# Graph attention on one Trainium2 core: score tiles of 256 nodes and eight heads in place of 128 nodes and sixteen, and an output of 64 matmuls of one form

## The chip, the cores and the metric

The kernel runs on one core of one Trainium2 chip. The core has five engines that run side by side: TensorE (matmuls; in profiles PE, and PEld for its loads of weights), VectorE (DVE), ScalarE (ACT), GpSimd (POOL) and SyncE (SP), which here only issues DMA transfers. SBUF is the on-chip memory, PSUM the banks that matmuls add into. The metric is the device time of one launch in microseconds, as a median of several runs. For a matmul the profile writes the form of the array that it uses, rows by weights: 128\*32 is a tile of all 128 rows and 32 weights, and four such tiles fill the array; 32\*64 and 32\*32 are smaller tiles, of which eight and sixteen fill it.

## The reference

Sixteen graphs (B) of 512 nodes (N) with 512 features. Every node attends to the first 20 nodes of its graph (ng), in two directions d, with 16 heads of 32 features; masks and biases come from 11 edge labels. Cut to what matters:

```python
def _gat_attention(self_feat, cond_adj, label_bias, Wq, bq, Wk, bk, Wout, bout):
    kv = self_feat[:, :ng]
    qh = (self_feat @ Wq.T + bq).reshape(B, N, H, dh)
    kh = (kv @ Wk.T + bk).reshape(B, ng, H, dh)
    aff = jnp.einsum('bnhd,bmhd->bnhm', qh, kh) * (1.0 / np.sqrt(dh))
    mask = cond_adj[:, :, None, :] > 0
    aff = jnp.where(mask, aff, NEG) + label_bias[:, :, None, :]
    w = jax.nn.softmax(aff, axis=-1)
    out_t = jnp.einsum('bnhm,bmf->bnhf', w, kv)
    out = jnp.einsum('bnhf,hgf->bnhg', out_t, Wout) + bout.reshape(H, F // H)
    return out.reshape(B, N, F)
...
self_feat = vcq @ W_self.T + b_self
output = self_feat
for d in range(2):
    A = adj_f if d == 0 else jnp.swapaxes(adj_f, 1, 2)
    A = A[:, :, :NONGT, :]
    cond = A.sum(-1)
    vb = A @ w_bias + b_bias
    output = output + _gat_attention(self_feat, cond, vb, Wq[d], bq[d], Wk[d], bk[d], Wout[d], bout[d])
rel = jax.nn.relu(output)
return exp_v + rel
```

All of it is in float32.

## The kernel before

A setup phase of roughly the first 90 us folds the weights. The keys of all graphs are multiplied with the query weights beforehand (`g`: for each graph and head, 19 vectors, the difference of each key to the first), the values with the output weights (`bd_d` in DRAM), the query bias gives one term for each head and key (`cq_d`). After that a loop runs over the graphs, `b`, and in each over four tiles of nodes, `nt`. Everything stands in an order written out by hand (`manual_schedule`), engine by engine; transfers that must not start too early are held `behind` an instruction.

For one graph the loop does this.

The self features `sf` (512 features by 512 nodes) come from seven block products (`product`, into the banks `ps_a`, `ps_c`, `ps_d`), which VectorE joins (`partial`, `joined`). They are made one graph ahead.

`scores(b, nt, g, bank)` multiplies self features by keys. A score tile has 128 partitions in four quarters of 32, and each quarter is a column tile of TensorE: in a matmul the weights are 32 nodes of `sf`, and 152 columns (4 heads, 2 directions, 19 keys) move past them. Before the change quarter `a` holds the heads 4a to 4a+3, and all four quarters hold the same 32 nodes; a tile thus holds 128 nodes and all sixteen heads, in two banks of two halves each.

`mask_mul`, `mask_count` and `mask_sum` make the additive mask `add` of 256 nodes, 128 nodes on the partitions and two such blocks side by side. A score tile needs the mask of each node in the partition and column where that node stands, so `mask_spread` copies it there on ScalarE into `both`: for each of the four quarters and each of four blocks of 32 nodes one copy of 32 partitions by 80, sixteen copies for 256 nodes. `full_add` (GpSimd) adds the mask and the bias term `cq` to a tile of 640 columns. `weigh` (VectorE) adds the scores from PSUM, takes the maximum and subtracts it; `expo` is ScalarE's exponential; `normal` sums (VectorE) and divides (GpSimd); `turn` is VectorE's transpose of 32 by 32 blocks into `wt`, after which the partitions hold keys.

`attend(b, banks)` is the output: `vd` holds the values as weights, `wt` moves past them, and the result lands in four banks `ps_o`. Of a row quarter (32 of the 128 partitions) come 4 heads. Each head has 40 keys in `wt`, so that heads lie across the blocks of 32: the blocks 1 and 3 belong to two heads each and are taken by matmuls of 64 weights, the others by matmuls of 32 weights. `finish` adds `sf` (VectorE, four additions), applies bias and relu (ScalarE); `residual` adds x (GpSimd) and `store` sends the result. The output of graph b-1 is made in graph b, in tile 2.

The last graph is handled apart: the self features plus bias plus x (`biased`) are put into the banks by an identity matmul (`put_self`), the output follows in two parts (384 nodes, then 128), and VectorE takes it out with a maximum against x (`end`), after which `send` stores it.

```python
for first, runs in ((True, ((1, 2, 1), (5, 2, 3))), (False, ((0, 1, 0), (3, 1, 2), (4, 1, 2), (7, 1, 4)))):
    for at, n, j in runs:
        for a in range(HL):
```

These three lines are the order of the output's matmuls: block of 32 values `at`, `n` such blocks (32 or 64 weights), column block `j` of `wt`, and innermost the row quarter `a`.

## Time and profile before

| what | value |
|---|---|
| runs shown | 580.59, 581.49, 582.52 us; median 581.49 |
| span of the profiled execution | 578.9 us (core 0, mean granted TensorE clock 0.998) |
| one graph in the middle of the loop | 30.5 us |
| transfers | 123.26 MB, mean 213 GB/s |

The page has one time for the profiled execution, its span, from the first to the last instruction; the runs' times are measured around the whole launch and are longer. In the profile's rows a group is written as line, engine, operation, output <- input, shapes and count. A row of the timeline gives start, duration, engine, line, operation and count, and in brackets how long the engine was idle before it and what ended that. PEld rows are the loads of weights, which run beside the matmuls. The duration of a matmul is modelled, the start is recorded, so that the distance from start to start is the safer reading.

```profile
PEclk9999999999999999999999999999999999999999
DMA  8998997867777767777676777566666766674404
```

The page's slices show that the clock was at full speed in all forty of them, and the DMA engines busy some 70% of the time.

### The profile page before, as it was taken

To read this page: it belongs to the slowest core of one execution; us is meant where nothing else is said; L and a number is where in the kernel's file an instruction comes from. 1 tells how busy PE (TensorE), PEld (TensorE's weight loads), DVE (VectorE), ACT (ScalarE), POOL (GpSimd) and SP (SyncE) were. 2 spreads that over 40 slices of the span, in tenths; PEclk is the share of its full clock that TensorE was granted. 3 is DMA by queue.
4 is the path that set the end of the run, shared out by engine and by line. 5 is a ranking of instruction groups with operands and counts; after the bars stand their busy time and mean duration, and the time that the engine had idled before them with its cause. 6 is when DMAs were issued, how large, how long until landed. Compare 5 with 4: busy or idle time off the path is not lost.

```text
span 578.9 us, 31006 instructions
## 1 busy us (share of the span) xinstructions
PE 572.2 (99%) x13508; PEld 434.1 (75%) x13508; DVE 492.9 (85%) x790; ACT 393.6 (68%) x1162; POOL 404.6 (70%) x383
## 2 busy tenths in 40 slices
PE   9999999999999999999999999999999999999996
PEld 6544458888878787878778787877887878787873
DVE  0675776979898989898999999898989898989896
ACT  1234554687878777778786868687887877777571
POOL 2726986658586776858585867776858677785874
PEclk9999999999999999999999999999999999999999
DMA  8998997867777767777676777566666766674404
GB/s 315 382 396 283 333 361 233 237 195 219 209 233 185 220 187 204 213 185 228 167 220 166 222 166 220 164 206 180 204 193 192 195 192 189 192 208 111 147 19 147
DMA packets 98788, 123.26 MB, mean 213 GB/s; under 512 B 18877, under 2 KB 66969, under 8 KB 96605
## 3 DMA queue, kind: packets, MB, share of 16 engines
q1 hardware_dynamic: 96268, 117.54, 67.8%
q0 software_dynamic: 1392, 2.43, 1.8%
q8 instruction: 106, 1.74, 1.3%
q10 hardware_dynamic: 992, 1.31, 0.6%
q14 instruction: 30, 0.24, 0.1%
HBM read 82.30 MB, written 40.24 MB: 212 GB/s over the span
## 4 chain that ended last, share of the span: by engine, by line
PE 98%; DVE 1%; issue 0%; DVEq 0%
PE ps_s L366 46%; PE ps_a L284 19%; PE ps_c L284 9%; PE ps_o L436 6%; PE ps_d L284 5%; PE ps_v L658 3%; PE ps_k L598 3%; PE ps_kv L541 1%; PE ps_o L813 1%; PE ps_warm L500 1%; PE ps_nz L214 0%; PE ps_s L355 0%; PE _g(2, 2, 0, 14, 16)0_845 L692 0%; PE _g(0, 2, 0, 14, 16)0_448 L692 0%; PE g(3, 2, 0, 14, 16)0_1055 L692 0%
## 5 line engine op out<-in xcount | busy, mean ns | idle before, releaser
L366 PEld LDWEIGHTS ps_s<-g,sf 128*32 128x32 f32 x8192 | 263.6, 110 | 21.9 <-issue 14.8
L366 PE MATMUL ps_s<-g,sf 128*32 128x152 f32 x8192 | 278.1, 293 | 0.7 <-issue 0.7
L338 ACT COPY both<-add 32x80 f32<-32x80 f32 x512 | 130.9, 256 | 60.9 <-DVE add L329 55.1
L418 POOL TENSOR_TENSOR s<-s,sm 128x640 f32<-128x640 f32 x63 | 80.4, 1275 | 96.8 <-DVE sm L417 52.5
L345 POOL TENSOR_TENSOR full<-cq,both 128x640 f32<-128x640 f32 x64 | 100.3, 1568 | 26.9 <-issue 20.9
L318 ACT ACTIVATE prod<-adj,wb_sb 128x80 f32<-128x80 int32 x330 | 112.4, 432 | 0.0
L393 ACT ACTIVATE s<-s 128x640 f32<-128x640 f32 x63 | 46.5, 738 | 56.0 <-DVE s L388 55.6
L450 POOL TENSOR_TENSOR o<-o,x 128x512 f32<-128x512 f32 x60 | 76.3, 1293 | 0.0
L380 DVE TENSOR_TENSOR full<-ps_s,full 128x608 f32<-128x608 f32 x63 | 48.6, 772 | 22.5 <-PE ps_s L366 19.4
L284 PE MATMUL ps_a<-t,ws_s 128*32 128x246 f32 x1024 | 59.8, 371 | 0.0
L416 DVE TENSOR_REDUCE sm<-s 128x32 f32<-128x640 f32 x63 | 50.8, 807 | 10.5 <-ACT s L393 10.3
L384 DVE TENSOR_REDUCE ps_s<-full 128x32 f32<-128x640 f32 x63 | 52.2, 828 | 2.2
L425 DVE STREAM_TRANSPOSE wt<-s 128x640 f32<-128x640 f32 x63 | 52.8, 838 | 0.6 <-POOL s L418 0.6
L388 DVE TENSOR_TENSOR s<-full,ps_s 128x640 f32<-128x640 f32 x63 | 51.5, 818 | 1.1
L290 DVE SCALAR_TENSOR_TENSOR sf<-nz,qw,ps_a 128x246 f32<-128x246 f32 x128 | 51.5, 443 | 0.1
L284 PEld LDWEIGHTS ps_a<-t,ws_s 128*32 128x32 f32 x1024 | 34.4, 110 | 16.8 <-issue 0.8
L329 DVE TENSOR_REDUCE add<-prod 128x80 f32<-128x960 f32 x32 | 36.8, 1150 | 7.4 <-ACT prod L318 4.0
L447 ACT ACTIVATE o<-o,bo 128x512 f32<-128x512 f32 x60 | 38.3, 713 | 0.6 <-DVE o L445 0.6
L249 POOL TENSOR_TENSOR t<-x,t 128x492 f32<-128x492 f32 x32 | 36.8, 1151 | 1.3
L436 PE MATMUL ps_o<-wt,vd 32*32 32x512 f32 (+5 forms) x816 | 36.9, 578 | 0.0
L249 POOL TENSOR_TENSOR t<-x 128x492 f32<-128x492 f32 x32 | 36.8, 1151 | 0.0
L445 DVE TENSOR_TENSOR o<-ps_o,sf 128x512 f32<-128x512 f32 x60 | 36.7, 668 | 0.0
(225 smaller groups left out, 715.8 us busy)
## 6 DMA issues: line engine op xcount, KB each, us to landing
g<-g_d SPq DMA_DIRECT2D x60, 304.0 KB
g_d<-st SPq DMA_DIRECT2D x16, 1064.0 KB
out_T<-o SPq DMA_DIRECT2D x60, 256.0 KB
xn<-in_xn SPq DMA_DIRECT2D x56, 256.0 KB
x<-in_xT SPq DMA_DIRECT2D x56, 256.0 KB
adj<-in_adj SPq DMA_DIRECT2D x60, 220.0 KB
nz<-nz_d SPq DMA_DIRECT2D x14, 256.0 KB
wk<-in_wkT SPq DMA_DIRECT2D x2, 1024.0 KB
```

What stands on the lines that cost most here:

```text
L249: done["xsum"] = nc.gpsimd.tensor_sub(t, one, two)
L284: nc.tensor.matmul(to, lhs, x[:, k], start=start, stop=stop, skip_group_check=n != 2)
L290: done["partial"] = nc.vector.scalar_tensor_tensor(to[:, i], nzs[b][:, half(l)], qw[:, 2 * f + i, b : b + 1], parts[b, "a"][i][:, :HN], AL ...
L318: nc.scalar.activation(p[:, :, l], a[:, :, l], AF.Identity, scale=wb_sb[:, l : l + 1])
L338: done["spread"] = nc.scalar.copy(adds[b, h][bass.ts(a, R), :, g], add[r].rearrange("p (t m) -> p t m", t=2))
L345: done["full"] = nc.gpsimd.tensor_add(f, cqs[b].unsqueeze(1).to_broadcast(shape), adds[b, nt // 2][:, nt % 2].unsqueeze(2).to_broadcast(sh ...
L366: nc.tensor.matmul(to, sfs[b][:, k, bass.ds(nt * P + (2 * g + j) * R, R)], of, start=(onto is None and k == 0 and (whole or j == 0)), stop ...
L384: nc.vector.tensor_reduce(mx, f, AX.X, ALU.max)
L418: done["normal"] = nc.gpsimd.tensor_mul(s, s, sm.unsqueeze(3).to_broadcast(full))
L425: nc.vector.transpose(wts[b][:, nt], s.rearrange("p a h m -> p (a h m)"))
L436: nc.tensor.matmul(banks[a][bass.ds(at // 2 * DH, n * DH)].rearrange("p (t n) -> p t n", n=32), vd[r, bass.ds(at * DH, n * DH)], wt[r, :, ...
L450: nc.gpsimd.tensor_add(o[:, c], o[:, c], xs[b][:, c])
```

## The change

A score tile now holds 256 nodes and eight heads. Quarter `a` takes the head group `a // 2 * 2 + nt % 2` and, of every block of 64 nodes, the half `a % 2`; the tiles 0 and 1 share the first 256 nodes, the tiles 2 and 3 the others. The count and size of the score matmuls stay. Since a half of the partitions now has one set of heads, with 64 consecutive nodes, the mask is copied in four pieces of 64 partitions by 80 for 256 nodes. `load_cq` brings the bias terms of eight heads to each half, in two transfers of 64 partitions in place of four of 32, and `load_values` the values of two head groups to each row quarter, four transfers as before, of twice the size.

The output has one form of matmul: 32 rows, 32 weights, 256 columns, for each of two blocks of a head (`i`), two head groups (`c`), four heads (`e`) and four row quarters (`a`). Bank `a` now holds what row quarter `a` gives: two head groups for every second block of 32 nodes. `finish` and the last graph's `end` therefore read and write runs of 32 elements (`spread_out`), and the last graph's steps are split where a bank changes from one head group to the other.

On TensorE, this is the middle of the output of one graph before the change (names: line, operation, output <- input, weights by columns):

```order
L436 MATMUL ps_o_0_3137<-wt_2508,vd_2989 64x512
L436 MATMUL ps_o_1_3138<-wt_2508,vd_2989 64x512
L436 MATMUL ps_o_2_3139<-wt_2508,vd_2989 64x512
L436 MATMUL ps_o_3_3140<-wt_2508,vd_2989 64x512
L436 MATMUL ps_o_0_3137<-wt_2508,vd_2989 32x512
L436 MATMUL ps_o_1_3138<-wt_2508,vd_2989 32x512
L436 MATMUL ps_o_2_3139<-wt_2508,vd_2989 32x512
L436 MATMUL ps_o_3_3140<-wt_2508,vd_2989 32x512
```

and this is where the output of one graph begins after it, with the product and the score tile ahead:

```order
L285 MATMUL ps_c_2201<-x_1608,ws_s 32x246 x16
L369 MATMUL ps_s_1_2385<-g_1960,sf_2061 32x152 x64
L443 MATMUL ps_o_0_2493<-wt_1850,vd_2359 32x256
L443 MATMUL ps_o_1_2494<-wt_1850,vd_2359 32x256
L443 MATMUL ps_o_2_2495<-wt_1850,vd_2359 32x256
L443 MATMUL ps_o_3_2496<-wt_1850,vd_2359 32x256
```

The 24 matmuls of two widths have become 64 of one width, half as many columns each, with the four banks still in turn; the stages around them stand where they stood.

On ScalarE, a stretch of the loop before:

```order
L193 ACTIVATE xn_1_2571,rs_2720<-xn_1_2571 128x512 x2
L338 COPY both_0_2733<-add_0_2731 32x2x40 x16
L393 ACTIVATE s_3_2852<-s_3_2852 128x640
L318 ACTIVATE prod_1_2866<-adj_1_2437,wb_sb 128x80 x11
L338 COPY both_1_2996<-add_1_2994 32x2x40 x8
L393 ACTIVATE s_0_3010<-s_0_3010 128x640
```

and the same stretch after:

```order
L194 ACTIVATE xn_1_2571,rs_2720<-xn_1_2571 128x512 x2
L338 COPY both_0_2733<-add_0_2731 64x2x40 x4
L396 ACTIVATE s_3_2840<-s_3_2840 128x640
L319 ACTIVATE prod_1_2854<-adj_1_2397,wb_sb 128x80 x11
L338 COPY both_1_2984<-add_1_2982 64x2x40 x2
L396 ACTIVATE s_0_2992<-s_0_2992 128x640
```

The copies of the mask stand at the same places, a quarter as many, each on 64 partitions.

The diff, cut to its core:

```diff
     def load_cq(b, ins=None):
-        cqs[b] = load.tile([P, HL, S], F32, tag="cq", name=f"cq{b}")
-        for a in range(HL):
+        cqs[b] = load.tile([P, 2, HL, S], F32, tag="cq", name=f"cq{b}")
+        for p in range(2):
             behind(nc.sync.dma_start(
-                cqs[b][bass.ts(a, R)].rearrange("p h m -> p (h m)"),
-                cq_d[b : b + 1, bass.ts(a, HL)].rearrange("b h d m -> b (h d m)").partition_broadcast(R),
-            ), ins if a == 0 else None)
+                cqs[b][bass.ts(p, P // 2)].rearrange("p c h m -> p (c h m)"),
+                cq_d[b : b + 1, bass.ts(p, H // 2)].rearrange("b h d m -> b (h d m)").partition_broadcast(P // 2),
+            ), ins if p == 0 else None)
...
-        vds[b] = gp.tile([P, HL, 2, DH], F32, tag="vd", name=f"vd{b}", bufs=1)
-        for c in range(C):
+        vds[b] = gp.tile([P, 2, HL, 2, DH], F32, tag="vd", name=f"vd{b}", bufs=1)
+        for a in range(HL):
+            of = bd_d[b >= EARLY][a // 2 * 2 : a // 2 * 2 + 2, b if b < EARLY else b - EARLY]
             behind(nc.sync.dma_start(
-                vds[b][bass.ts(c, 32)].rearrange("p e i g -> p (e i g)"), bd_d[b >= EARLY][c, b if b < EARLY else b - EARLY].rearrange("r e i g -> r (e i g)")
-            ), ins if c == 0 else None)
+                vds[b][bass.ts(a, R)].rearrange("p c e i g -> p c (e i g)"), of.rearrange("c r e i g -> r c (e i g)")
+            ), ins if a == 0 else None)
...
         done["masks"] = nc.vector.tensor_reduce(add, prods.pop((b, h)), AX.X, ALU.add)
-        adds[b, h] = msk.tile([P, 2, HL, S], F32, tag="both", name=f"both{b}_{h}")
+        adds[b, h] = msk.tile([P, 2, 2, S], F32, tag="both", name=f"both{b}_{h}")
...
         for a in quarters:
-            for g in range(HL):
-                r = bass.ts(g, R)
-                done["spread"] = nc.scalar.copy(adds[b, h][bass.ts(a, R), :, g], add[r].rearrange("p (t m) -> p t m", t=2))
+            p, u = bass.ts(a // 2, P // 2), a % 2
+            done["spread"] = nc.scalar.copy(
+                adds[b, h][p, :, u], add[bass.ts(u, P // 2)].rearrange("p (t m) -> p t m", t=2)
+            )
...
         done["full"] = nc.gpsimd.tensor_add(
-            f, cqs[b].unsqueeze(1).to_broadcast(shape),
-            adds[b, nt // 2][:, nt % 2].unsqueeze(2).to_broadcast(shape),
+            f, cqs[b][:, nt % 2].unsqueeze(1).to_broadcast(shape),
+            adds[b, nt // 2].rearrange("p t u m -> p (t u) m").unsqueeze(2).to_broadcast(shape),
         )
...
                 for a in range(HL):
-                    to, of = bank[bass.ts(a, R), bass.ts(j, WD // HL)], keys[:, k, a]
+                    at = nt // 2 * 2 * P + (2 * g + j) * 2 * R + a % 2 * R
+                    to, of = bank[bass.ts(a, R), bass.ts(j, WD // HL)], keys[:, k, a // 2 * 2 + nt % 2]
                     if onto is not None:
...
                     nc.tensor.matmul(
-                        to, sfs[b][:, k, bass.ds(nt * P + (2 * g + j) * R, R)], of,
+                        to, sfs[b][:, k, bass.ds(at, R)], of,
                         start=(onto is None and k == 0 and (whole or j == 0)), stop=(k == C - 1 and (whole or j == 1)),
...
         if nt == 0:
-            wts[b] = work.tile([P, NT, W], F32, tag="wt", name=f"wt{b}")
-        nc.vector.transpose(wts[b][:, nt], s.rearrange("p a h m -> p (a h m)"))
-
-    def attend(b, banks, tiles=slice(0, NT), start=True, stop=True):
-
-
-        wt = wts[b][:, tiles].rearrange("p t (g w) -> p (t g) w", g=HL)
-        vd = vds[b].rearrange("p e i g -> p (e i g)")
-        for first, runs in ((True, ((1, 2, 1), (5, 2, 3))), (False, ((0, 1, 0), (3, 1, 2), (4, 1, 2), (7, 1, 4)))):
-            for at, n, j in runs:
-                for a in range(HL):
-                    r = bass.ts(a, R)
-                    nc.tensor.matmul(
-                        banks[a][bass.ds(at // 2 * DH, n * DH)].rearrange("p (t n) -> p t n", n=32),
-                        vd[r, bass.ds(at * DH, n * DH)], wt[r, :, bass.ts(j, 32)],
-                        start=start and first, stop=stop and not first,
-                    )
+            wts[b] = work.tile([P, 2, 2, W], F32, tag="wt", name=f"wt{b}")
+        nc.vector.transpose(wts[b][:, nt % 2, nt // 2], s.rearrange("p a h m -> p (a h m)"))
+
+    def spread_out(t, a):
+
+        return t[:, a // 2 * 2 : a // 2 * 2 + 2].rearrange("p c (n u r) -> p c u n r", u=2, r=R)[:, :, a % 2]
+
+    def attend(b, banks, spans, start=True, stop=True):
+
+
+        for i in range(2):
+            for c, at, lo, hi in spans:
+                for e in range(HL):
+                    for a in range(HL):
+                        r = bass.ts(a, R)
+                        wt = wts[b][:, c, lo:hi].rearrange("p l (g w) -> p (l g) w", g=HL)
+                        nc.tensor.matmul(
+                            banks[a][bass.ts(e, DH), bass.ds(at, (hi - lo) * P)].rearrange("p (n r) -> p n r", r=R),
+                            vds[b][r, c, e, i], wt[r, :, bass.ts(e * S // 32 + i, 32)],
+                            start=start and i == 0 and at == 0, stop=stop and i == 1, skip_group_check=True,
+                        )
...
-        for c in range(C):
-            done["add", c] = nc.vector.tensor_add(o[:, c], banks[c], sfs[b][:, c])
+        for a in range(HL):
+            done["add", a] = nc.vector.tensor_add(
+                spread_out(o, a), banks[a].rearrange("p (c n r) -> p c n r", c=2, r=R), spread_out(sfs[b], a)
+            )
         for c in range(C):
...
     with tc.manual_schedule():
-        def put_self(banks, lo, hi, q):
-
-            nc.tensor.matmul(
-                banks[q][:, : (hi - lo) * P], ident, biased[:, q, lo * P : hi * P], start=True, stop=False
+        def put_self(bank, a, ns):
+
+            for lo in range(ns.start, ns.stop, N // 2):
+                n = min(N // 2, ns.stop - lo)
+                nc.tensor.matmul(
+                    bank[:, bass.ds(lo - ns.start, n)], ident, biased[:, a, bass.ds(lo, n)],
+                    start=lo == ns.start, stop=False, skip_group_check=True,
+                )
+
+        def put_bias(c):
+            nc.scalar.activation(
+                biased[:, c // 2 * 2 : c // 2 * 2 + 2].rearrange("p u (c n r) -> p n c u r", c=2, r=R)[:, :, c % 2],
+                sfs[b][:, c].rearrange("p (n u r) -> p n u r", u=2, r=R), AF.Identity, bias=bo[:, c : c + 1],
             )
+
+        def add_x(a, lo):
+            for c in range(2):
+                at = slice(max(lo, c * N // 2), (c + 1) * N // 2)
+                if at.start < at.stop:
+                    nc.gpsimd.tensor_add(
+                        biased[:, a, at].rearrange("p (n r) -> p n r", r=R),
+                        biased[:, a, at].rearrange("p (n r) -> p n r", r=R),
+                        spread_out(xs[b], a)[:, c, at.start // R - c * 8 :],
+                    )
...
                         for c in (0, 1):
-                            nc.gpsimd.tensor_add(biased[:, c], biased[:, c], xs[b][:, c])
+                            add_x(c, 0)
                     if b > 0:
                         banks = [bank(f"ps_o{b - 1}_{q}", q) for q in range(4)]
-                        attend(b - 1, banks)
+                        attend(b - 1, banks, ((0, 0, 0, 2), (1, N // 2, 0, 2)))
                         o = work.tile([P, C, N], F32, tag="o", name=f"o{b - 1}")
...
                     for q in range(4):
-                        put_self(most, 0, NT - 1, q)
+                        put_self(most[q], q, slice(0, N - P))
                     s = soft.tile(full, F32, tag="s", name=f"s{b}_{nt}", bufs=3)
...
         rest += [bank(f"ps_o{b}_{q}_2", q - 2) for q in (2, 3)]
-        for lo, hi, banks in ((0, NT - 1, most), (NT - 1, NT, rest)):
-            if banks is rest:
-                for q in range(4):
-                    put_self(rest, lo, hi, q)
-            attend(b, [t[:, : (hi - lo) * P] for t in banks], slice(lo, hi), False)
-
-        def end(lo, hi, banks, q):
-
-            ns = slice(lo * P, hi * P)
-            nc.vector.tensor_max(o_last[:, q, ns], banks[q][:, : (hi - lo) * P], xs[b][:, q, ns])
-
-        def send(queue, c, lo, hi, n=2):
-            queue.dma_start(out_b[:, c : c + n, lo * P : hi * P], o_last[:, c : c + n, lo * P : hi * P])
-
-        w = (NT - 1) * P
-        nc.scalar.activation(o_last[:, 3, :w], most[3][:, :w], AF.Relu)
-        behind(nc.gpsimd.tensor_add(o_last[:, 3, :w], o_last[:, 3, :w], xs[b][:, 3, :w]), done["half"])
-        for q in range(3):
-            end(0, NT - 1, most, q)
-            send(nc.scalar if q == 1 else nc.sync, q, 0, NT - 1, 1)
-        send(nc.scalar, 3, 0, NT - 1, 1)
-        for q in range(4):
-            end(NT - 1, NT, rest, q)
-            if q % 2:
-                send(nc.scalar if q == 1 else nc.sync, q - 1, NT - 1, NT)
+        attend(b, most, ((0, 0, 0, 2), (1, N // 2, 0, 1)), False)
+        for a in range(HL):
+            put_self(rest[a], a, slice(N - P, N))
+        attend(b, rest, ((1, 0, 1, 2),), False)
+
+        pieces = ((0, 0, 8, 0), (1, 0, 4, N // 2))
+        last = (1, 4, 8, 0)
+
+        def end(bank, a, piece):
+
+            c, lo, hi, at = piece
+            nc.vector.tensor_max(
+                spread_out(o_last, a)[:, c, lo:hi],
+                bank[:, bass.ds(at, (hi - lo) * R)].rearrange("p (n r) -> p n r", r=R),
+                spread_out(xs[b], a)[:, c, lo:hi],
+            )
+
+        def send(queue, q, lo=0, hi=N):
+            queue.dma_start(out_b[:, q, lo:hi], o_last[:, q, lo:hi])
+
+        for c, lo, hi, at in pieces:
+            to = spread_out(o_last, 3)[:, c, lo:hi]
+            nc.scalar.activation(to, most[3][:, bass.ds(at, (hi - lo) * R)].rearrange("p (n r) -> p n r", r=R), AF.Relu)
+            behind(nc.gpsimd.tensor_add(to, to, spread_out(xs[b], 3)[:, c, lo:hi]), done["half"])
+        for a in range(2):
+            for piece in pieces:
+                end(most[a], a, piece)
+        send(nc.sync, 0)
+        send(nc.scalar, 1, 0, N // 2)
+        for piece in pieces:
+            end(most[2], 2, piece)
+        send(nc.sync, 2)
+        send(nc.scalar, 3, 0, N // 2)
+        for a in range(HL):
+            end(rest[a], a, last)
+            if a % 2:
+                send(nc.scalar if a == 1 else nc.sync, a, N // 2, N)
```

10 lines of the change are left out of this document (5 added, 5 removed).

## The prediction

> **What bounds the kernel now.** I read the page first, then the chain of waits, then the stages.
>
> ```profile
> span 578.9 us, 31006 instructions
> ...
> PE 572.2 (99%) x13508; PEld 434.1 (75%) x13508; DVE 492.9 (85%) x790; ACT 393.6 (68%) x1162; POOL 404.6 (70%) x383
> ...
> PE 98%; DVE 1%; issue 0%; DVEq 0%
> ```
>
> TensorE is busy throughout and is 98% of the chain. A busy TensorE need not be one at its peak, so the question is how long each stage takes against its columns. The chain over one batch item, and the same stretch by engine (length, then PE, PEld, DVE, ACT and POOL busy, clock, DMA share, GB/s):
>
> ```profile
> 311.55 2.17 PE ps_o L436 x48
> 313.72 4.27 PE ps_s L366 x128
> 318.00 1.66 PE ps_a L284 x32
> 319.65 1.66 PE ps_d L284 x32
> 321.31 1.66 PE ps_a L284 x32
> 322.98 4.13 PE ps_s L366 x128
> ...
> 342.03 2.17 PE ps_o L436 x48
> ```
>
> ```profile
> 311.55:342.03 30.48, 30.48 (x793) 24.21 (x795) 27.83 (x43) 23.47 (x71) 22.06 (x20) 1.00 0.71 191
> ```
>
> An item takes 30.48 us, TensorE works in all of them, at full clock, and VectorE for 27.83. So only what shortens or lengthens TensorE's own stages counts, as long as VectorE's queue keeps up. The change touches one such stage, the output of 2.17 us (ps_o). The scores keep count and shape: 64 matmuls of 32 weights by 152 columns a tile, before and after.
>
> **What a column costs.** Each matmul of the program runs as two passes in the trace, and four column tiles run side by side: the product of 1.66 us is 32 records, 8 passes of 246 columns, 0.2075 us each, 0.843 ns a column. The output stage, in order of time:
>
> ```profile
> 311.48 0.23 PEld L436 LDWEIGHTS ps_o<-wt,vd 32*64 32x64 f32 x16 [0.24 <-issue]
> 311.48 2.24 PE L436 MATMUL ps_o<-wt,vd 32*64 32x512 f32 x48
> 312.52 0.29 PEld L436 LDWEIGHTS ps_o<-wt,vd 32*32 32x32 f32 x32 [0.81 <-issue]
> 313.65 4.03 PEld L366 LDWEIGHTS ps_s<-g,sf 128*32 128x32 f32 x128 [0.84 <-issue]
> ```
>
> Eight matmuls with 64 weights fill the array first (16 loads), then sixteen with 32 weights (32 loads). From load to load the first group holds the array for 1.04 us and the second for 1.13. Two passes of 512 columns are 2 x 512 x 0.843 = 0.863 us, so the groups carry 0.18 and 0.27 us beyond their columns. In both, the loads end early (0.23 and 0.29 us) and then stand idle for 0.81 and 0.84 us, until the form of tile changes. The kernel's last two output stages test this:
>
> ```profile
> 570.41 0.23 PEld L436 LDWEIGHTS ps_o<-wt,vd 32*64 32x64 f32 x16 [0.55 <-DVE mx L399]
> ...
> 572.15 0.97 PEld L813 LDWEIGHTS ps_o<-biased,ident 128*128 128x128 f32 x8 [0.62 <-issue]
> ...
> 573.24 0.96 PE L436 MATMUL ps_o<-wt,vd 32*64 32x128 f32 x48
> 573.64 0.29 PEld L436 LDWEIGHTS ps_o<-wt,vd 32*32 32x32 f32 x32 [0.17 <-issue]
> ```
>
> With 384 columns the stage takes 1.74 us, 0.43 less than with 512; four passes of 128 columns are 4 x 128 x 0.843 = 0.43. So it is column time plus a constant 0.44 us.
>
> **The output part, the one that moves the sum.** Now 64 matmuls of 256 columns, all of one form, 32 rows by 32 weights. A tile of the array gets 4 matmuls, 8 passes of 256 columns: 8 x 256 x 0.843 = 1.73 us, the column time of before. What goes is the change from 64 to 32 weights in the middle, the 0.18 us; the 0.27 us of sixteen staggered tiles and the change to the scores' form stays. I take 2.00 us, a gain of 0.17 to 0.18. Bounds: 1.73 (nothing beyond columns) and, from above, the row of 48 records in 0.96 us, 20 ns each, 128 x 20 = 2.56 us. I lean to the low end because that 0.96 still holds a change of form, and because the 32 loads of 0.29 us come at 9 ns each, while the columns need one in 1.73/128 = 13.5 ns. By the Trainium skill, TensorEngine Tiling (Array Packing), section Key Properties, a change of tiling mode drains the array; by that rule the middle gap goes with its change, and the load's idle time before each change agrees.
>
> How often it counts:
>
> ```profile
> 127.90 2.68 PE ps_o L436 x46
> ...
> 555.38 2.17 PE ps_o L436 x48
> ```
>
> There are 15 full output stages from the first to the last of these. After the last, VectorE's queue sets the pace:
>
> ```profile
> 555.52 0.79 DVE L380 TENSOR_TENSOR full<-ps_s,full 128x608 f32<-128x608 f32 x1 [0.26 <-PE ps_s L366]
> ...
> 562.18 0.73 DVE L380 TENSOR_TENSOR full<-ps_s,full 128x608 f32<-128x608 f32 x1
> ```
>
> It works without a break from 555.52, begun by scores older than that output stage, to the next weighing at 562.18. So I count 14: 14 x 0.18 = 2.5 us.
>
> **Mask copies.**
>
> ```profile
> L338 ACT COPY both<-add 32x80 f32<-32x80 f32 x512 | 130.9, 256 | 60.9 <-DVE add L329 55.1
> L393 ACT ACTIVATE s<-s 128x640 f32<-128x640 f32 x63 | 46.5, 738 | 56.0 <-DVE s L388 55.6
> ```
>
> 128 copies for 512, still 80 elements a partition: 384 x 0.256 = 98 us off ScalarE. They lie beside TensorE. The exponentials that follow them wait for VectorE, not for ScalarE (55.6 of 56.0 us), so earlier copies release nothing: 0. The additions that read the masks (L345) keep shape and count.
>
> **VectorE.** The four additions an item that take the output out of PSUM now read and write runs of 32 elements:
>
> ```profile
> L445 DVE TENSOR_TENSOR o<-ps_o,sf 128x512 f32<-128x512 f32 x60 | 36.7, 668 | 0.0
> L380 DVE TENSOR_TENSOR full<-ps_s,full 128x608 f32<-128x608 f32 x63 | 48.6, 772 | 22.5 <-PE ps_s L366 19.4 <-issue 3.1
> L290 DVE SCALAR_TENSOR_TENSOR sf<-nz,qw,ps_a 128x246 f32<-128x246 f32 x128 | 51.5, 443 | 0.1
> ```
>
> L380 adds PSUM to SBUF in runs of 19 and costs 772/608 = 1.27 ns an element, L445 1.30: I take no change. L290, the dearest neighbour, has 1.80 ns, which would be 0.92 us for one addition. Where a delay would strike:
>
> ```profile
> 319.85 0.84 DVE L290 SCALAR_TENSOR_TENSOR sf<-nz,qw,ps_a 128x246 f32<-128x246 f32 x2
> ...
> 321.13 1.85 PE L284 MATMUL ps_a<-t,ws_s 128*32 128x246 f32 x32
> ```
>
> The sixth product adds to a bank that VectorE has just read, until 320.69; TensorE comes at 321.13. The output stage lies ahead on both engines' ways, and VectorE's way (weighing, transpose, four additions, sums, weighing, L290) has no break. So 0.44 us of slack, 0.26 after a gain of 0.18. It holds.
>
> **Transfers.**
>
> ```profile
> vd<-bd_d SPq DMA_DIRECT2D x64, 32.0 KB
> ...
> cq<-cq_d SPq DMA_DIRECT2D x64, 20.0 KB
> ```
>
> ```profile
> 335.21 1.76 SPq L141 DMA_DIRECT2D vd<-bd_d  x4
> ```
>
> The values double (four of 64 KB an item), the query terms double in two transfers of 80 KB in place of four of 20. That is 0.2 MB more in an item that moves 191 GB/s x 30.48 us = 5.8 MB at a DMA share of 0.71. The values are issued 6.8 us ahead of the output stage at 342.03; the mask and x loads behind them on SP's queue start no later, since the number of issues does not grow. 0, hidden by that slack.
>
> **The end.** VectorE finishes in 10 steps, not 7:
>
> ```profile
> L1049 DVE TENSOR_TENSOR o<-ps_o,x 128x384 f32<-128x384 f32 x3 | 1.4, 535 | 0.0
> ...
> L1049 DVE TENSOR_TENSOR o<-ps_o,x 128x128 f32<-128x128 f32 x4 | 0.9, 284 | 0.0
> ```
>
> ```profile
> 572.82 2.36 DVE L1049 TENSOR_TENSOR o<-ps_o,x 128x384 f32<-128x384 f32 x7
> ```
>
> Three of 384 columns become three of 256 and three of 128. By the two rows 256 columns cost 284 + (535 - 284)/2 = 410 ns, so 3 x (410 + 284 - 535) = 0.48 us more; the row of 7 takes 2.36 and not their sum 2.74, an overlap of 0.06 a step, so 0.3. The extra identity matmuls and the two shorter output stages lie ahead of VectorE's 572.82 and do not set the end. Bounds 0 and 0.5; I take 0.3.
>
> **Sum.** 578.9 - 2.5 + 0.3 = 576.7 us of span. The median of the runs shown, 581.49, is 2.6 us above the profiled span; I keep that: 579.3 us.
>
> **The rivals.**
>
> *The gap stays* (chance 0.10). If the 0.18 us belongs to starting tiles and not to the change of form, the stage remains at 2.17 and only the end's 0.3 is left: 581.8. For it: the trace has no output stage of one form. Against: with 384 columns the constant was the same, and the loads stood idle up to the change.
>
> *Too many short matmuls* (0.15), the slower side. Issue decides once one pass with its load costs more than 13.5 ns. At the 20 ns of the short last stage, 2.56 us, 0.39 more, 15 times, and the end: 581.5 + 5.9 + 0.3 = 587.7. For it: sixteen tiles with several rounds each never run in this trace, and the program gets 40 more matmuls an item. Against: loads at 9 ns. The Trainium skill, TensorE: Matmul & The Clock Gate, Part 1, section Wait — 56ns, not 53.3ns?, says start to start never drops below about 25 ns. By that rule the stage would take 128 x 25 = 3.2 us and the kernel 581.5 + 15 x 1.03 + 0.3 = 597.3, an estimate from the page; the 48 records in 0.96 us already go below it, so I give that figure no weight of its own.
>
> *VectorE late at the sixth product* (0.05), slower too. It decides from 0.11 us more an addition (0.44/4). At L290's price, 4 x 0.25 = 1.0 us late, 0.56 beyond the slack of before, 14 times: 581.5 + 7.8 + 0.3 = 589.6. Against: L380's price for shorter runs.
>
> *More gain* (0.06): the stagger shrinks too and the stage comes to 1.73, 0.44 less, 14 times: 575.6. Against: sixteen tiles must still start one after another and the scores' form must still come.
>
> **How the numbers follow.** The forecast holds 0.64; its own range, with 0.10 to 0.27 us of gain a stage, is 578.0 to 580.4. A difference of 0.3% (1.74 us, about what a measurement of this kernel can tell from none) puts the line at 579.75; three quarters of the forecast lies below. Faster: 0.48 + 0.06 = 0.54. Same: 0.16 + 0.10 = 0.26. Slower: 0.20. The range goes from 577 to 587: it leaves out most of the fourth rival, the dear end of the second and the third, some 0.15.
>
> **What would show it.** In the chain, ps_o pieces of 2.00 us with 128 records, between scores of 4.13 and 4.27 as before; an item of 30.3 us; loads of the output in one form, without an idle gap in the middle. ps_o at 2.17 shows the first rival, at 2.5 the second. The third shows as idle time of TensorE's loads ahead of ps_a, put down to VectorE, and in a mean of the additions well over 668 ns. ScalarE's copies at 128 x 0.256 = 33 us with no change elsewhere show that they were off the path. I would be wrong at the root if the scores' 4.13 us moved.

## The result and the profile after

The changed kernel takes 609.71 us (median of 6 runs, 606.12 to 613.07) beside 581.09 us of the kernel before in the same session: a ratio of 1.0495, 95% interval 1.0468 to 1.0522. In a second session (run 9 below) it took 602.06 beside 581.00, a ratio of 1.0364, interval 1.0322 to 1.0405. It is 5.0% slower in the one session and 3.6% in the other; the prediction had 579.3 us and a range from 577 to 587.

The page of the changed kernel, the rows that answer to those of before:

```profile
span 605.9 us, 33188 instructions
...
PE 588.0 (97%) x14812; PEld 483.5 (80%) x14812; DVE 497.0 (82%) x793; ACT 296.0 (49%) x779; POOL 404.0 (67%) x387
...
q8 instruction: 116, 1.90, 1.4%
...
PE 97%; issue 2%; DVE 1%; DVEq 0%
...
L369 PE MATMUL ps_s<-g,sf 128*32 128x152 f32 x8192 | 287.6, 294 | 5.0 <-issue 5.0
...
L338 ACT COPY both<-add 64x80 f32<-64x80 f32 x128 | 32.9, 257 | 56.4 <-DVE add L330 55.1
L443 PE MATMUL ps_o<-wt,vd 32*32 32x256 f32 (+1 forms) x2112 | 48.3, 379 | 6.9 <-issue 6.9
...
L452 DVE TENSOR_TENSOR o<-ps_o,sf 128x512 f32<-128x512 f32 x60 | 36.9, 673 | 3.5 <-PE ps_o L443 3.4
```

Two things are new. The page's chain of waits holds 2% "issue" where there was none: TensorE stood still and nothing that the profile shows released it. This idle time stands before matmuls of the output (6.9 us) and of the scores (5.0). And the queue that brings instructions moved 116 packets, 1.90 MB: 16 KB each. TensorE shows 14812 loads and 14812 matmuls, which over 116 packets are 255 a packet. So a packet holds about 256 instructions of TensorE (the places of the stops, below, show that it is 256), and one matmul of the program is four of them (two passes, each a load and a matmul).

The rest is as it was. ScalarE's copies fell to 32.9 us and nothing came of it; the additions out of PSUM cost 673 ns for 668.

The chain over a graph without such a stop (start, length, what):

```profile
484.73 2.69 PE ps_o L443 x116
487.42 4.27 PE ps_s L369 x128
491.69 1.66 PE ps_a L285 x32
...
496.70 4.13 PE ps_s L369 x128
...
515.75 0.33 PE ps_o L443
```

and over the beginning of one with the longest:

```profile
256.31 2.50 PE ps_o L443 x95
258.81 2.12 issue
260.93 0.69 PE ps_o L443 x21
261.61 5.95 PE ps_s L369 x128
267.56 1.66 PE ps_a L285 x32
```

So there are two losses. The output takes 2.69 us where it took 2.17, in every graph; scores and products have the lengths of before. And TensorE stops in most graphs, in the output or in the scores right behind it.

In the graph with the longest stop the scores behind it also took 5.95 us where they take 4.27. That is the clock. The row of the whole graph (length, then each engine's busy time, clock, DMA share, GB/s) has a mean granted clock of 0.95:

```profile
256.23:291.52 35.29, 33.17 (x868) 26.72 (x864) 28.20 (x43) 17.33 (x47) 21.94 (x20) 0.95 0.68 186
```

The trace's record of the clock has 0.5 from 262.32 to 265.73 us, which lies in these scores, and 1.0 in the rest of the loop. Those 3.41 us at half speed cost 1.7, and 4.27 + 1.7 is 5.97. Run 5 below has the same once; in the other executions the clock stays at 1.0 in the loop, also in this one after stops of 2.08 and 2.02 us, so no run shows which stop brings it.

The stretch from the first to the fifteenth output, which leaves setup and end aside (length, then each engine's busy time, clock, DMA share, GB/s), before:

```profile
127.85:555.31 427.46, 427.46 (x10978) 339.90 (x10977) 391.17 (x605) 328.78 (x994) 309.43 (x266) 1.00 0.69 191
```

and after, with one graph that has no stop:

```profile
126.23:580.94 454.71, 442.87 (x12100) 388.68 (x12096) 394.72 (x605) 243.74 (x656) 309.12 (x268) 1.00 0.66 187
```

```profile
484.66:515.68 31.02, 31.02 (x866) 26.50 (x865) 28.08 (x43) 17.39 (x47) 22.02 (x20) 1.00 0.67 197
```

The stretch grew by 27.2 us, of 27.0 in the span. A graph without a stop takes 31.01 us for 30.47, which is 14 x 0.54 = 7.5 us. What is left, 454.7 - 14 x 31.01 = 20.6 us, are the stops and what follows them, 1.7 us of it the halved clock; the kernel before has 0.9 us by the same reckoning.

### The profile page after: what moved, and what is told of

The parts are those of the page before. It is cut to its first block, busy times and chain, and to the rows that moved or that the text cites. A ratio compares the mean times of both kernels' runs of the same rounds, so it can differ in the third digit from the quotient of the medians.

```text
span 605.9 us, 33188 instructions
## 1 busy us (share of the span) xinstructions
PE 588.0 (97%) x14812; PEld 483.5 (80%) x14812; DVE 497.0 (82%) x793; ACT 296.0 (49%) x779; POOL 404.0 (67%) x387
## 3 DMA queue, kind: packets, MB, share of 16 engines
q0 software_dynamic: 1392, 2.43, 1.7%
## 4 chain that ended last, share of the span: by engine, by line
PE 97%; issue 2%; DVE 1%; DVEq 0%
PE ps_s L369 45%; PE ps_a L285 18%; PE ps_c L285 9%; PE ps_o L443 8%; PE ps_d L285 4%; PE ps_v L667 3%; PE ps_k L607 3%; PE ps_kv L550 1%; PE ps_o L824 1%; PE ps_warm L509 1%; PE ps_nz L215 0%; PE ps_s L357 0%; PE _g(2, 2, 0, 14, 16)0_837 L701 0%; PE _g(0, 2, 0, 14, 16)0_448 L701 0%; PE g(3, 2, 0, 14, 16)0_1041 L701 0%
## 5 line engine op out<-in xcount | busy, mean ns | idle before, releaser
L369 PE MATMUL ps_s<-g,sf 128*32 128x152 f32 x8192 | 287.6, 294 | 5.0 <-issue 5.0
L369 PEld LDWEIGHTS ps_s<-g,sf 128*32 128x32 f32 x8192 | 269.4, 110 | 20.9 <-issue 14.8
L285 PE MATMUL ps_a<-t,ws_s 128*32 128x246 f32 x1024 | 63.0, 371 | 0.0
L338 ACT COPY both<-add 64x80 f32<-64x80 f32 x128 | 32.9, 257 | 56.4 <-DVE add L330 55.1
L443 PE MATMUL ps_o<-wt,vd 32*32 32x256 f32 (+1 forms) x2112 | 48.3, 379 | 6.9 <-issue 6.9
L285 PEld LDWEIGHTS ps_a<-t,ws_s 128*32 128x32 f32 x1024 | 43.3, 110 | 9.7 <-issue 0.2
L443 PEld LDWEIGHTS ps_o<-wt,vd 32*32 32x32 f32 x2112 | 30.0, 103 | 21.4 <-issue 13.7
```

Of the source, the lines that this page charges most:

```text
L285: nc.tensor.matmul(to, lhs, x[:, k], start=start, stop=stop, skip_group_check=n != 2)
L369: nc.tensor.matmul(to, sfs[b][:, k, bass.ds(at, R)], of, start=(onto is None and k == 0 and (whole or j == 0)), stop=(k == C - 1 and (whol ...
L443: nc.tensor.matmul(banks[a][bass.ts(e, DH), bass.ds(at, (hi - lo) * P)].rearrange("p (n r) -> p n r", r=R), vds[b][r, c, e, i], wt[r, :, b ...
```

## The experiments

The theories, as the expectations name them. F, the prediction's: the first 0.18 us of the output belong to its change of form. R: a round of matmuls over sixteen tiles of the array costs some 0.19 us beyond its columns, because only so many instructions can be under way. I: instructions arrive too slowly. T: data transfers delay them. C: the fewer mask copies do, by moving other work. In the table, "unstopped graph" is the shortest distance between two outputs, "stops" is the loop stretch less 14 of them, and "256 instructions" is the shortest time in which TensorE starts 256 of its instructions in a row, all worked out from the recorded starts of each profiled execution.

| run | median us | before, same session | ratio (95%) | output us | unstopped graph | stops | 256 instructions |
|---|---|---|---|---|---|---|---|
| kernel before | 581.09 | | | 2.17 | 30.47 | 0.9 | 4.02 |
| the change | 609.71 | 581.09 | 1.0495 (1.0468 to 1.0522) | 2.69 | 31.01 | 20.6 | 2.58 |
| 1 output 32 x 512 | 582.33 | 580.88 | 1.0033 (1.0013 to 1.0053) | 2.28 | 30.58 | 0.2 | 3.70 |
| 2 output 64 x 256 | 598.98 | 580.88 | 1.0325 (1.0286 to 1.0365) | 2.69 | 30.99 | 10.4 | 2.57 |
| 3 40 tiny, dense | 603.48 | 580.88 | 1.0394 (1.0364 to 1.0425) | 2.17 | 31.21 | 12.2 | 2.18 |
| 4 change, 48 | 588.99 | 580.88 | 1.0137 (1.0099 to 1.0176) | 2.48 | 30.78 | 4.3 | 3.35 |
| 5 40 tiny, sparse | 596.96 | 579.50 | 1.0297 (1.0275 to 1.0320) | 2.17 | 31.20 | 6.5 | 2.80 |
| 6 change, 8 tiles | 608.15 | 579.50 | 1.0482 (1.0436 to 1.0528) | 3.45 | 31.75 | 8.4 | 3.27 |
| 7 as 2, values doubled | 597.43 | 579.50 | 1.0302 (1.0272 to 1.0332) | 2.69 | 30.99 | 11.4 | 2.57 |
| 8 change, no stores | 600.52 | 579.50 | 1.0354 (1.0315 to 1.0393) | 2.69 | 31.35 | 9.0 | 2.57 |
| 9 the change again | 602.06 | 581.00 | 1.0364 (1.0322 to 1.0405) | 2.69 | 30.99 | 11.7 | 2.57 |
| 10 as 2, again | 598.83 | 581.00 | 1.0320 (1.0290 to 1.0349) | 2.69 | 30.99 | 11.0 | 2.57 |
| 11 change, 16 copies | 603.34 | 581.00 | 1.0389 (1.0355 to 1.0424) | 2.69 | 30.99 | 16.0 | 2.43 |

In run 8 no graph was free of stops; with the 30.99 us of its like, its stops are 14.1. Run 12 is told below.

**Run 1.** The kernel before, its output in one form of 512 columns:

```diff
-        for first, runs in ((True, ((1, 2, 1), (5, 2, 3))), (False, ((0, 1, 0), (3, 1, 2), (4, 1, 2), (7, 1, 4)))):
-            for at, n, j in runs:
+        for i in range(2):
+            for e in range(HL):
                 for a in range(HL):
...
-                        banks[a][bass.ds(at // 2 * DH, n * DH)].rearrange("p (t n) -> p t n", n=32),
-                        vd[r, bass.ds(at * DH, n * DH)], wt[r, :, bass.ts(j, 32)],
-                        start=start and first, stop=stop and not first,
+                        banks[a][bass.ts(e, DH)].rearrange("p (t n) -> p t n", n=32),
+                        vd[r, bass.ts(2 * e + i, DH)], wt[r, :, bass.ts(e * S // 32 + i, 32)],
+                        start=start and i == 0, stop=stop and i == 1,
```

> The kernel before, with its output in 32 matmuls of 32 weights and 512 columns, all of one form, in place of 8 with 64 weights and 16 with 32; nothing else differs. Theory F (that of the prediction: the 0.18 us of the first group go with its change of form): output stage about 2.00 us, 0.17 less, 14 or 15 times, 579 us against 581 of the kernel before. Theory R (every round of matmuls over sixteen tiles of the array costs some 0.19 us beyond its columns, whatever the form; two rounds here): 2 x (0.43 + 0.43 + 0.19), and 0.1 for the scores' form, 2.2 us, so no gain: 581 to 582. Theory I (the instructions of the output and the scores behind it arrive too slowly in their 16 KB packets): 32 more instructions a graph, a small loss at most, 581 to 584.

Its chain:

```profile
311.50 2.28 PE ps_o L436 x62
313.78 4.27 PE ps_s L366 x128
...
342.08 2.29 PE ps_o L436 x62
```

The change of form is gone and the stage is 0.11 us longer, not 0.17 shorter. Theory F falls; R's 2.2 holds to 0.08 us. The starts of TensorE's matmuls, in us from a point just ahead of the output, show what took the place of the change of form:

```
before (8 matmuls of 64 weights, then 16 of 32):
  first of 64: 0.032 (2nd pass 0.512)       first, second of 32: 1.077, 1.083
run 1 (two rounds of 16, 512 columns):
  round 1: 0.028, 0.034 (2nd pass 0.484)    round 2: 0.913, 1.106
the change (four rounds of 16, 256 columns):
  round 1: 0.057, 0.064 (2nd pass 0.300)
  round 2: 0.517, 0.709   round 3: 1.163, 1.356   round 4: 1.810, 2.002
```

From round to round the first matmul starts when its tile is free, and the second 0.19 us later, although its own tile, started 7 ns after the first, should be free 7 ns after it. From then on matmuls start every 17 ns instead of 7. Run 1 loses 0.19 us in this way to its second round; the change has three such places, and its rounds are 0.646 us apart for 2 x 256 x 0.843 = 0.432 us of columns.

The kernel before has no second round over sixteen tiles, and its starts divide the 0.18 us of its first group. The second pass comes 0.480 us after the first for 0.432 of columns, 0.05 over; the eight starts are spread over another 0.05; and from the last start of the old form (0.559) to the first of the new (1.077) are 0.518 us, 0.09 over a pass. Only these 0.09 stand at the change of form itself.

**Run 2.** The kernel before, its output in the change's count and size, in the old layout:

```diff
+        count = wts[b][:, tiles].shape[1] * HL
+        half = 8 if count > 8 else count
+        for i in range(2):
+            for lo in range(0, count, half):
+                hi = min(lo + half, count)
+                for e in range(HL):
+                    for a in range(HL):
+                        r = bass.ts(a, R)
+                        nc.tensor.matmul(
+                            banks[a][bass.ts(e, DH), bass.ds(lo * 32, (hi - lo) * 32)].rearrange("p (t n) -> p t n", n=32),
+                            vd[r, bass.ts(2 * e + i, DH)], wt[r, lo:hi, bass.ts(e * S // 32 + i, 32)],
+                            start=start and i == 0 and lo == 0, stop=stop and i == 1, skip_group_check=True,
+                        )
```

> The kernel before, with its output in 64 matmuls of 32 weights and 256 columns, all of one form: the count, size and form of the changed kernel, in the old layout, with the old mask copies, transfers and additions. If all the loss lies in the output's form and count (theories R and I together), it is as slow as the changed kernel, 605 to 612 us. If the loss were round sixteen tiles alone (R): four rounds, stage 2.69 us, 0.52 more 15 times, 589 us. If the layout, the transfers or VectorE made the loss, it stays at 581 to 584.

```profile
320.62 2.69 PE ps_o L440 x116
...
351.81 2.69 PE ps_o L440 x116
```

The output's form and count alone make 18 us: the same 2.69 us, and stops. Theory R alone (589) is too little. The 10 us between this run and the changed kernel led to runs 7 to 11.

**Run 3 and run 5.** The kernel before with 40 matmuls of four columns more in each graph, so that it has the change's number of instructions; in run 3 right behind the output, in run 5 ahead of the second block product.

```diff
+                        for n in range(40):
+                            nc.tensor.matmul(
+                                ps[0][bass.ts(n % HL, R), :4], sfs[b][:, 0, :R], gs[b][:, 0, :4], start=True, stop=True,
+                            )
                     for g in range(2):
                         scores(b, nt, g, ps[g])
```

```diff
+        if n == 2 and b:
+            for m in range(40):
+                nc.tensor.matmul(
+                    parts[b, "d"][bass.ts(m % HL, R), :4], ws_s[:, 0, 0, :R], x[:, 0, :4], start=True, stop=True,
+                )
         for i in range(2):
             for k in range(2):
```

> The kernel before, with 40 matmuls of 32 weights by 4 columns more in each graph, behind the output and ahead of the next scores, into a bank that those scores overwrite: as many instructions as the changed kernel, 160 more a graph, and hardly a column more. By themselves 40 such matmuls, 80 passes in the trace, at 9 to 20 ns are 0.7 to 1.6 us a graph, 15 times: 592 to 605 without any stop. Theory I: beside that, stops of 0.4 to 2.5 us in the output or the scores behind it, each ending some 1.3 us after a packet of instructions has landed, as in the changed kernel: 8 to 20 us more, 600 to 620. Theory R: no such stops, the output stage stays at 2.17 and the time follows from the matmuls alone.

> The kernel before with the same 40 matmuls of 32 weights by 4 columns more in each graph as in the run with them behind the output, but now between two of the block products (ahead of the second, into its bank), where 64 instructions take 1.66 us. As many instructions a graph as that run and the changed kernel. Theory I: what counts is how fast 256 instructions are used up, not their number; here no 344 instructions in a row take less than about 5.5 us (5.7 in the kernel before, 4.0 in the changed one), so no stops: 30.47 + 0.74 us an item, 15 times 0.74, 592 us. If the number of instructions or the tiny matmuls themselves made the loss: 603 us as with them behind the output.

The chain of run 3:

```profile
352.23 2.17 PE ps_o L436 x48
354.40 0.81 PE ps_s L942 x54
355.20 2.10 PE ps_s L366 x60
357.30 1.27 issue
358.57 2.39 PE ps_s L366 x66
```

and of run 5:

```profile
318.96 2.17 PE ps_o L441 x48
321.13 4.27 PE ps_s L371 x128
325.41 1.65 PE ps_a L289 x30
327.05 0.68 PE ps_d L271 x52
327.73 1.72 PE ps_d L289 x32
```

Forty matmuls with hardly a column cost 0.74 us of their own in both places, and in run 3 another 12.2 us of stops, in a kernel whose output is untouched. Moved among the products the stops are 6.5 us, 3.4 of them in one graph, where half is again the clock (0.5 from 264.36 to 267.77 us, after a stop of 1.75). So the place counts, as theory I says, but my figure of none was wrong: I had reckoned 5.5 us for any 344 instructions in a row, and by the recorded starts the tightest such stretch is 4.2.

**Where the stops stand.** Numbering all of TensorE's recorded instructions (loads, matmuls and the few semaphore instructions) by their starts, each stop of the changed kernel falls on the same place of a packet. Some of them, with the packet of the instruction queue that landed last:

```
idle from  to      us    in      number mod 256  packet landed  start after landing
128.88  130.97   2.08   output       193            129.72          1.25
164.07  164.87   0.80   scores       193            163.46          1.41
258.44  260.93   2.49   output       193            259.40          1.53
295.12  297.14   2.02   scores       193            295.67          1.47
422.24  423.57   1.33   output       193            422.23          1.34
550.25  551.66   1.41   output       193            550.28          1.38
```

The number of packets landed by then is, in every row, the number of the packet at whose bound the engine stood. Over all fourteen profiled executions (before, after and twelve runs) there are 81 gaps of more than 0.56 us between two starts in the loop (a pass of 512 columns leaves 0.52), and all 81 stand at number 193; where a stop ended, work began 1.1 to 1.6 us after the landing. In the kernel before the packets land at least 1.5 us ahead of their first instruction. The one that came so late stands before a gap of 0.34 us, at number 193 too (226.85 us); no other gap at a bound there is over 0.2, so the kernel before had little to spare.

The same records show how far ahead the packets come: one. In all fourteen loops a packet's transfer starts at the earliest 0.7 us before TensorE starts on the packet ahead of it, and at the latest 3.9 us after that. In the kernel before it has landed 0.5 to 3.2 us after that moment (median 1.8), in the change after 0.4 to 4.0 (median 2.3). So a packet that is used up faster than the next one is begun, moved (0.9 to 2.6 us) and taken up leaves TensorE without instructions.

**Run 4.** The changed kernel, with the blocks that two heads share taken with 64 weights, 48 matmuls:

```diff
-        for i in range(2):
+        for first, runs in ((True, ((1, 2, 1), (5, 2, 3))), (False, ((0, 1, 0), (3, 1, 2), (4, 1, 2), (7, 1, 4)))):
             for c, at, lo, hi in spans:
-                for e in range(HL):
+                vd = vds[b][:, c].rearrange("p e i g -> p (e i g)")
+                for v, n, j in runs:
                     for a in range(HL):
```

> The changed kernel, with its output in 48 matmuls of 256 columns: blocks that two heads share are taken with 64 weights as before the change, the others with 32; layout, mask copies and the rest as changed. Theory R: the 64-weight rounds go over eight tiles and lose less, stage about 2.4 us, 589 to 600 with the stops that remain. Theory I: 64 instructions a graph fewer, 1664 against 1728, so fewer or shorter stops; 585 to 600 with both. If the layout made the loss: as the changed kernel, about 609.

```profile
348.28 2.48 PE ps_o L444 x92
350.75 4.27 PE ps_s L369 x128
```

589.0 us, 8 above the kernel before. The loop has 14 x 0.31 = 4.3 us of stage and 4.3 of stops, and that is all of its growth (7.7 us, with the 0.9 of before); layout, copies, transfers and additions leave nothing in it. Its starts show both kinds of wait next to each other: four passes over eight tiles 0.216 us apart (0.288, 0.504, 0.720 from the second on), which is 256 x 0.843 and no more, then 0.304 from the last start of that form to the first of the next (0.09 over the pass), then 1.527 and 1.721 in the second round over sixteen tiles. By the Trainium skill, TensorEngine Tiling (Array Packing), section Key Properties, a change of mode drains the array; this run agrees with a price of 0.09 us at 256 columns, the same as in the kernel before at 512.

**Run 6.** The changed kernel, the 64 matmuls in two phases of eight tiles; half of the array is idle in each.

```diff
-        for i in range(2):
-            for c, at, lo, hi in spans:
-                for e in range(HL):
+        for i, spans_of, es in [(i, [s], es) for es in ((0, 1), (2, 3)) for i in range(2) for s in spans]:
+            for c, at, lo, hi in spans_of:
+                for e in es:
```

> The changed kernel with its 64 output matmuls in another order: first the heads 0 and 1 (eight tiles of the array), then the heads 2 and 3 (the other eight), so that half of the array is idle and each phase has four rounds over eight tiles. Theory R in the form that only some 64 instructions can be under way: with eight tiles no round waits, the passes follow each other at 0.216 us, 16 of them, stage 3.5 to 3.6 us. Rival: every new use of a 32-weight tile costs 0.19 us, whatever the number of tiles in use: 8 rounds of 0.62, stage 5.0 us. Time: 581 + 15 x 1.4 = 602 and what stops remain, fewer than in the changed kernel since 256 instructions now take 3.6 us, so 602 to 612; by the rival 623 and more.

```profile
356.54 3.45 PE ps_o L443 x124
359.99 4.27 PE ps_s L369 x128
...
388.30 3.45 PE ps_o L443 x123
```

3.45 us is 16 passes of 0.216: with eight tiles no round waits, in the same form of matmul, so the 0.19 us is a matter of how many tiles are in use at once, as R has it; why sixteen wait is not shown. A round over sixteen tiles is 64 instructions. The Trainium skill, TensorE: Matmul & The Clock Gate (table at its head), gives TensorE a queue 64 deep; the traces fit that, for a wait begins when a second round would follow 64 instructions still under way, but no run here varies the number apart from the tiles. The order costs more columns than it saves waits.

**Runs 7 to 11.** What makes the changed kernel slower than its output form alone? Run 7 is run 2 with the change's loads of the values; run 8 the changed kernel without the output transfers of graphs 0 to 14, but for one block; run 9 the changed kernel unaltered; run 10 run 2 once more; run 11 the changed kernel with each mask copy made four times.

```diff
+        vds[b] = gp.tile([P, 2, HL, 2, DH], F32, tag="vd", name=f"vd{b}", bufs=1)
+        for a in range(HL):
+            of = bd_d[b >= EARLY][a // 2 * 2 : a // 2 * 2 + 2, b if b < EARLY else b - EARLY]
...
-                            vd[r, bass.ts(2 * e + i, DH)], wt[r, lo:hi, bass.ts(e * S // 32 + i, 32)],
+                            vds[b][r, a % 2, e, i], wt[r, lo:hi, bass.ts(e * S // 32 + i, 32)],
```

```diff
         for b, c, o in outs:
-            nc.sync.dma_start(out[b, bass.ts(c, P)], o[:, c])
+            if c == 0 and b == 0:
+                nc.sync.dma_start(out[b, bass.ts(c, P)], o[:, c])
```

```diff
-            done["spread"] = nc.scalar.copy(
-                adds[b, h][p, :, u], add[bass.ts(u, P // 2)].rearrange("p (t m) -> p t m", t=2)
-            )
+            for rep in range(4):
+                done["spread"] = nc.scalar.copy(
+                    adds[b, h][p, :, u], add[bass.ts(u, P // 2)].rearrange("p (t m) -> p t m", t=2)
+                )
```

> The kernel before with its output in 64 matmuls of 256 columns, as in the run that had that alone, and in addition the changed kernel's loads of the values (four transfers of 64 KB for four of 32), of which the output uses the half that it needs. Theory T: the changed kernel's stops are longer than those of the 64 matmuls alone because its larger transfers ahead of the output delay the instruction packets; then this run comes to 603 to 610 us. If the transfers do not matter: as the 64 matmuls alone, 597 to 602.

> The changed kernel without the output transfers of graphs 0 to 14 (except one block of 256 KB), 1 MB of some 5.8 MB an item; the results of these graphs stay in SBUF. Theory T: the instruction packets wait for other transfers, so less traffic makes the stops shorter: 590 to 604 us. If the packets' delay has nothing to do with the traffic: 606 to 613 us as the changed kernel.

> The changed kernel itself, on the chip of the next three runs. Theory I: its loss beyond the stage (2.69 us, 15 times 0.52) is made of stops that depend on when packets land, so that it differs a little from one execution and chip to the next: 600 to 613 us.

> The kernel before with its output in 64 matmuls of 256 columns once more, beside the changed kernel on one chip. If the 10 us between the two (599 and 610) are the chip's or chance, they meet here; if something else of the change adds to the stops, the changed kernel stays 6 to 12 us slower.

> The changed kernel with each copy of a mask made four times, so that ScalarE has as many copies as before the change (512). Theory C: fewer copies let ScalarE's later work and with it the transfers held behind it start earlier, and these then meet the instruction packets; with the copies back the stops shrink to those of the 64 matmuls alone, 597 to 602 us. If ScalarE's copies do not matter: as the changed kernel on this chip, within 3 us.

In one session the changed kernel (602.06, ratio 1.0322 to 1.0405) and its output form alone (598.83, ratio 1.0290 to 1.0349) overlap: most of the 10 us lay between sessions, not between kernels; a remainder of some 3 us can't be told from none. The values' larger transfers add nothing that can be told (597.4, ratio 1.0302 for run 2's 1.0325), nor do the mask copies when they come back (603.3). Run 8 looked like a gain of 9 us until run 9 gave the same ratio without it, so no run settles whether other transfers delay the packets. The traces only hint at it: of the 1310 packets in the fourteen loops, those with the DMA engines under 40% busy in the 2 us after TensorE began the packet ahead landed 1.4 us after that moment in the median, at 40 to 90% 2.0 to 2.1, above that 2.6.

**Run 12.** The changed kernel with 32 matmuls of four columns more in the setup.

```diff
             for _ in range(7):
                 nc.tensor.matmul(warm[:, :P], ones, ones, start=True, stop=True)
+            for _ in range(32):
+                nc.tensor.matmul(warm[:, :4], ones, ones[:, :4], start=True, stop=True)
```

> The changed kernel with 32 matmuls of 4 columns more in the setup, in a stretch where TensorE waits for data: 128 instructions, half a packet, so that the packets' bounds fall at other places of each graph. Theory I: every stop still stands at a packet's bound (instruction 193 of 256 by the records), now at other places of the graph, and the time moves by some us either way, 596 to 616. If the stops belonged to places of the program (a buffer, a semaphore, a transfer of data), they stay at the same matmuls and the time stays within 2 us.

618.45 us, ratio 1.0636 (1.0597 to 1.0675). But these 32 took 14 us of setup, which I had taken for idle. By line, the loads and the matmuls of it (shortest, median and longest in ns, first and last start):

```profile
L511 PEld LDWEIGHTS ps_warm<-ones x64: 333/333/333, 4.0 to 17.4; 128*128 128x128 f32 x64
L511 PE MATMUL ps_warm<-ones x64: 214/354/354, 4.2 to 17.5; 128*128 128x4 f32 x64
```

The loop from the first to the fifteenth output takes 446.8 us, beside 445.5 in run 9; these are the two, run 12 first:

```profile
141.84:588.64 446.80, 440.91 (x12098) 392.57 (x12097) 394.17 (x605) 243.63 (x656) 309.19 (x268) 1.00 0.66 190
```

```profile
127.44:572.97 445.53, 440.92 (x12097) 387.21 (x12096) 394.42 (x605) 243.75 (x656) 309.12 (x268) 1.00 0.65 191
```

What the run tells is where the stops are. Counting instructions from the first matmul of a graph's output to the stop, in the graphs where both kernels stop for over 0.38 us:

```
output no.           3          4     6     10    14
run 9 (the change)   361        415   268   227   187
run 12 (+128)        233, 489   287   395   355   59, 315
```

Every stop of run 12 stands again at number 193 of a packet, and within the graph it has moved by 128 instructions (127 in one graph), one way or the other: half a packet. The stops belong to the packets' bounds, not to a matmul, a buffer or a transfer. Their sum hardly changed: 12.9 us over 14 x 30.99, beside 11.7 in run 9.

No run beat the kernel before. The nearest, run 1, takes 0.1 to 0.5% more.

## Why the prediction was wrong

**The output part** is the step that failed. It put the 0.18 us ahead of the 32-weight matmuls down to the change of form and let it go with that. By the recorded starts only half of it, 0.09 us, stands at the change of form; and run 1 shows that a round over sixteen tiles that follows another costs 0.19, so nothing is won by one form. Halving the columns makes three such places. The term was -0.18 us an output, measured +0.52 to 0.54: 7.5 us over the loop in place of -2.5. The rows shown then could not tell the two apart, because before the change no round over sixteen tiles followed another. The bound from above, 2.56 us from 20 ns a record, was exceeded (2.69).

**The rival of too many short matmuls** named the 40 matmuls more in a graph but priced TensorE's issue only, by the time between starts. It said 587.7; the stage it gives (2.56) is near. That issue as such is no bound is shown by starts 7 ns apart over eight tiles (run 4) and by the 80 passes of the tiny matmuls in run 3, which start within 0.74 us, 9 ns apart. In the later rounds over sixteen tiles, though, starts come 17 ns apart, more than the rival's 13.5, and no run separates that pace from the wait of 0.19 us ahead of it. The same starts speak against the 25 ns start to start of the Trainium skill, TensorE: Matmul & The Clock Gate, Part 1, section Wait — 56ns, not 53.3ns?, for matmuls on different tiles; it would have given 597.3.

**The rival of the gap that stays** was right that one form wins nothing, though part of the 0.18 us is the form's, but it knew nothing of a wait for each further round; it said 581.8, close to what run 1 takes (582.3).

**What no part had** are the stops, 12 to 21 us, which the sum put at nothing. The page of before carried the row: 106 instruction packets for TensorE's 27016 loads and matmuls. Four instructions a matmul, 64 matmuls in 2.69 us: 256 instructions, a whole packet, in 2.6 us, where the tightest 256 of before took 4.02. In the fourteen executions two packets never start less than 3.27 us apart, and the medians in the loop lie between 4.5 and 5.0. Output and the scores after it are 512 instructions in 2.69 + 4.27 us, so a packet that is a little late shows. The Trainium skill, Runtime: NRT & Kernel Launch, section Instruction fetch mechanics, has the blocks of 16 KB and 256 instructions, as measured here, and calls crossing a bound mostly hidden; that holds for the kernel before and not for this one.

**The other steps held.** Mask copies: 128 x 257 ns = 32.9 us and no gain; run 11 makes them 512 again without a loss that can be told. VectorE: 673 ns for 668, and no wait of the sixth product on it. Transfers: run 7. Scores and products kept 4.13, 4.27 and 1.66 us. The end: from the beginning of the last output to the last instruction 8.5 us before, 9.2 after and 8.6 in run 9, so 0.2 to 0.7 for the 0.3 forecast.

Two things stay open: what sets the delay of a single packet, and so why the same kernel's stops were 20.6 us in one profiled execution (1.7 of them the clock) and 11.7 in another; and what it is in a further round over sixteen tiles that makes it wait.

## What to carry to other kernels

Count instructions as well as columns: a float32 matmul is four for TensorE here, and a kernel that uses up 256 of them faster than they arrive stops at packets' bounds, however well everything else is hidden. In these runs a kernel whose tightest 256 took 3.70 us or more lost next to nothing (run 1, the kernel before), and those with 3.35 us and less lost 4 to 21 us (run 4 and the others). The page's row of the instruction queue and the count of loads and matmuls tell how near a kernel is; splitting matmuls in two doubles the count at the same columns. And a wait that seems to belong to a feature (here a change of form) may only stand where another would stand without it: test it by removing the feature alone.

## What was not expected of the hardware

Instruction packets of 256 limit TensorE here: all 81 gaps above 0.56 us lie at one number of 256, TensorE goes on 1.1 to 1.6 us after the packet landed, and packets come only one ahead. As few as 40 matmuls of four columns a graph, 0.74 us of work, cost 12 us more of stops where the code is dense. Sixteen 32 by 32 tiles in rounds lose about 0.2 us a round (0.646 us apart for 0.432), eight lose nothing (passes 0.216 us apart for 0.216 us of columns). The clock was halved for 3.4 us in two of the fourteen loops, each time after a stop. And a matmul of four columns with a full tile of 128 by 128 weights cost 0.43 us in the setup (13.8 us for 32); that run's record of the clock begins only after them, at 22.5 us, so their clock is not known.
